# A layer in front of a scan: one affine operation a block into an image in DRAM, and the convolution's row windows loaded from that image

## The chip, the cores and the metric

The kernel runs on one core of a Trainium2 chip. The metric is the device time of one execution in microseconds (us). The core has a matrix engine (PE, whose weight loads are shown apart as PEld), a vector engine (DVE), a scalar engine (ACT), a general engine (POOL), and a queue engine (SP), which here issues nearly all DMA transfers. Each engine works through its own list of instructions in order; between engines, semaphores hold an instruction back until what it needs is there. All data is 32-bit floating point.

## The reference

The input is four images of 128 channels by 128 x 128 pixels. Four layers follow, each `x = x + layer(groupnorm(x))`:

- layer 0, a deformable 3x3 convolution (offsets and a mask from a small convolution, bilinear samples gathered from the image, then a projection);
- layer 1, a dilated 5x7 convolution to 16 channels and two 1x1 convolutions;
- layer 2, described below;
- layer 3, a 3x3 convolution less a term of differences of the channel sum.

Layer 2 is the one that matters here:

```python
x = cf_layernorm(x, pre_w, pre_b)          # over the channels of a pixel
x1, x2 = jnp.split(x, 2, axis=1)           # two halves of 64 channels
x1 = dwconv(x1, dw_w)                      # 3x3, one filter a channel
x2 = ss2d(x2.transpose(0, 2, 3, 1), ...)   # in_proj, 3x3 dwconv, silu, a selective scan
                                           # in four directions, a norm, a gate, out_proj
y = jnp.stack([x1, x2], axis=2).reshape(Bb, 2 * C, a, b)
return cf_layernorm(y, post_w, post_b)
```

The selective scan walks over all 16384 pixels of an image in four orders (by rows, by columns, and both backwards), with 16 states for each of 128 channels. That recurrence is the largest piece of work of the whole program.

## The kernel before

An image is held in DRAM between the layers as 128 channels (partitions) by 16384 pixels. Work goes by blocks of `R = 4` rows, `N = 512` pixels; an image has `NBLK = 32` blocks.

**The scan and what runs beside it.** `scan` is the main loop: for every image, direction and block 16 steps, each one `tensor_tensor_scan` on DVE (L1092) over 128 partitions by 512 pixels, 8192 in all. A step needs a decay `pa`, which ACT computes with one `Exp` from `delta` (`decay`, L979) into one of two or three buffers, and its input `h`, which DVE (three times a block, L949) or POOL (once a block) makes from `du`. POOL multiplies the result with `cb` (`outputs`, L1016), and PE sums it. The tiles `delta`, `du`, `bb` and `cb` are loaded by SP once a block (L929, L936, L955, L961), spread over partitions, from small images in DRAM that the same loop has stored shortly before (`prepare`: `stepsd`, `bcd`).

All other layers of the images run beside that scan. They are Python generators: `weave` takes a list of groups of steps, each with a lag in blocks, and gives one round per block, with a `yield` after every group; the scan pulls so many groups after each of its own steps that both end together. For layer 2's first part this is about two groups a scan step, and a round has 27 groups. This fixes the order of the instructions on each engine when the program is built, and `keep_order` at the end holds it. `store` does not issue a DMA at once: it puts it on a list, and `tick`, called once after every scan step, counts its delay down and issues it on SP; `flush` issues all that wait. Any two DMAs of SP leave in program order, and one that must wait holds those behind it.

**Layer 2's first part, `layer2_pre`**, makes what the scan needs. Per block, with its lag in rounds in brackets:

- `fetch` (0) loads the block `xr`, `centre` (2) subtracts the channel mean with a matmul, `square` (2) copies the result `d` and its square out on ACT, `spread_variance` (3) averages the square over channels with a matmul, `invert` (3) makes the inverse root with `Ln` and `Exp` on ACT, `scale` (3) multiplies `d` by it on POOL (L713).
- `affine(-1)`, `affine(0)`, `affine(1)` (4; L737) apply the norm's weight and bias on ACT and put the result into the convolution's windows. A block has two windows of `R + 2` rows, `a` for the channels of the scan and `b` for the others; each holds its 64 channels twice, in the upper and the lower 64 partitions, one copy being a row further down, so that one matmul over 128 partitions does two rows of filter taps at once. `affine(0)` writes the block's own four rows, `affine(-1)` and `affine(1)` write its first and last row into the windows of the blocks before and after it. Each writes 64 partitions into `a` and 64 into `b`, so an inner block costs six operations on ACT.
- `shift` (5) has SP copy each window's half, `R + 1` rows, into the other half of the partitions, one row further down (L147, `win<-win`).
- `convolve` (6; L762, L765) runs six and three matmuls over the windows, `copy` (6; L774, L778) and `gate` (6; L785) take the results and project the gate `z`, and `finish_strip` (6) applies Silu to two blocks at once, with two loads of ACT's function tables, and stores `u`, `z` and a transposed copy of `u`.

For image 0 the stage starts with nothing beside it, since the scan can't begin before its first blocks are there; for images 1 to 3 it runs beside the scan of the image before.

Of the kernel before, what the change touches and what calls it, by code (L numbers as in the profile page):

```python
# [10 lines left out]
F32 = mybir.dt.float32  # L11
I32 = mybir.dt.int32
U32 = mybir.dt.uint32
AF = mybir.ActivationFunctionType
# [4 lines left out]
P = 128  # L19
H = 128  # L20
W = 128
HW = H * W
R = 4
N = R * W
NBLK = H // R
# [4 lines left out]
HALF = P // 2  # L30
# [17 lines left out]
V_PREW, V_PREB, V_POSTW, V_POSTB, V_CONVB, V_ONW, V_ONB, V_B3 = range(8)  # L48
# [40 lines left out]
MORE = None  # L89


def weave(n, order, ready=lambda t: True):


    total = n + max(step[0] for group in order for step in group if step is not MORE)
    for t in range(total):
        while not ready(t):
            yield None
        left = iter(())
        for k, group in enumerate(order):  # L100
            for step in group:
                if step is MORE:
                    next(left, None)
                elif 0 <= t - step[0] < n:
                    more = step[1](t - step[0])
                    left = left if more is None else more
            yield (t + (k + 1) / len(order)) / total
        for _ in left:
            pass
# [3 lines left out]
def conv_preact_kernel(ctx: ExitStack, tc: tile.TileContext, a: dict, nb: int):  # L113
    nc = tc.nc
# [4 lines left out]
    dram = ctx.enter_context(tc.tile_pool(name="dram", bufs=2, space=DRAM))  # L119
# [3 lines left out]
    def load(pool, src, shape, name, **kw):  # L123
        t = pool.tile(shape, F32, name=name, **kw)
        nc.sync.dma_start(t, src)
        return t

    def bank(which, name):
        return psb.tile([P, N], F32, name=name, tag=f"bank{which}")
# [4 lines left out]
    def store(dst, src, after=3, of=None):  # L134

        waiting.append([after, of, dst, src])

    def stored(of):
        return all(w[1] is not of for w in waiting)
# [9 lines left out]
    def flush():  # L149
        while waiting:  # L150
            nc.sync.dma_start(*waiting.pop(0)[2:])
# [13 lines left out]
    vec = load(const, a["vec"], [P, NVEC], "vec_sb")  # L165

    def col(i):
        return vec[:, i : i + 1]
# [10 lines left out]
    zero = const.tile([P, 2 * P], F32, name="zero")  # L179
# [18 lines left out]
    def slots(n):  # L198
        for _ in range(n):
            yield None  # L200
# [4 lines left out]
    def rows_of(t, y, n):  # L205

        return t[:, y * W : (y + n) * W].rearrange("p (r w) -> p r w", w=W)

    def flat(t):
        return t.rearrange("p r w -> p (r w)")  # L210

    def rsqrt(dst, src, eps):
        nc.scalar.activation(dst, src, AF.Ln, bias=eps)
        nc.scalar.activation(dst, dst, AF.Exp, scale=-0.5)

    def gn_affine(stats, which=0):

        both = bank(which, "pmv")
        mv = small.tile([P, 2], F32, name="mv")
        nc.vector.bn_aggr(mv, stats)  # L220
        yield from slots(2)
        pm = both[:, 0:1]
        nc.tensor.matmul(pm, gmat, mv[:, 0:1], start=True, stop=True)
        yield None
        d = small.tile([P, 1], F32, name="gnd")
        nc.vector.tensor_sub(d, mv[:, 0:1], pm)
        e = small.tile([P, 1], F32, name="gne")
        nc.vector.scalar_tensor_tensor(e, d, d, mv[:, 1:2], ALU.mult, ALU.add)
        yield from slots(2)
        pv = both[:, 1:2]  # L230
        nc.tensor.matmul(pv, gmat, e, start=True, stop=True)
        yield None
        sc = small.tile([P, 1], F32, name="gnscale")
        rsqrt(sc, pv, gn_eps)
        yield None
        sh = small.tile([P, 1], F32, name="gnshift")
        nc.vector.scalar_tensor_tensor(sh, pm, -1.0, sc, ALU.mult, ALU.mult)
        yield None
        return sc, sh
# [4 lines left out]
    def image(name, parts=P):  # L244
        return dram.tile([parts, HW], F32, name=name)
# [404 lines left out]
    def layer2_pre(st):  # L650
        CH = 32
        x2d, stats = st["x2"], st["stats2"]
        zd, yd = image("zd"), image("yd")
        urow, ucol = image("urow"), image("ucol")
        st["z"], st["y1"], st["u"], st["out"] = zd, yd, (urow, ucol), 0
        low = slice(0, HALF)
        with ExitStack() as s:
            wp = s.enter_context(tc.tile_pool(name="l2w", bufs=1))
            pp = s.enter_context(tc.tile_pool(name="l2p", bufs=2))
            inx = load(wp, a["inx"], [P, P], "inx_sb")  # L660
            inz = load(wp, a["inz"], [P, P], "inz_sb")
# [9 lines left out]
            for t in range(6):  # L671
# [2 lines left out]
                nc.vector.tensor_scalar_mul(diag[:, t % 3, half], eye2, dww[:, t : t + 1])  # L674
                yield None
            nc.sync.dma_start(yd[HALF:P, (H - 1) * W :], zero[HALF:P, 0:W])
            sc, sh = yield from gn_affine(stats)

            cms = wp.tile([P, P], F32, name="cms")
# [8 lines left out]
            got = {}  # L688
# [23 lines left out]
                d = got["d", i]  # L712
                nc.gpsimd.tensor_mul(d, d, got.pop(("s", i)))  # L713

            def window(i):

                if ("w", i) not in got:
                    got["w", i] = a, b = [
                        pp.tile([P, R + 2, W], F32, name=f"win{h}", bufs=4) for h in range(2)
                    ]  # L720
                    for edge, row in ((0, 0), (NBLK - 1, R + 1)):
                        if i == edge:
                            nc.gpsimd.memset(a[HALF:P, row, :], 0.0)
                            nc.gpsimd.memset(b[low, row, :], 0.0)
                return got["w", i]

            def affine(to_block):

                to = {0: slice(1, R + 1), -1: slice(R + 1, R + 2), 1: slice(0, 1)}[to_block]
                of = {0: slice(0, R), -1: slice(0, 1), 1: slice(R - 1, R)}[to_block]  # L730

                def one(i):
                    d = got["d", i].rearrange("p (r w) -> p r w", w=W)
                    if not 0 <= i + to_block < NBLK:
                        return
                    for t, part in zip(window(i + to_block), (slice(HALF, P), low)):
                        nc.scalar.activation(  # L737
                            t[part, to, :], d[part, of, :], AF.Identity,
                            bias=vec[part, V_PREB : V_PREB + 1], scale=vec[part, V_PREW : V_PREW + 1],
                        )  # L740

                return one

            def shift(i):
                a, b = got["w", i]
                store(a[low, 1 : R + 2, :], a[HALF:P, 0 : R + 1, :], 2, a)
                store(b[HALF:P, 1 : R + 2, :], b[low, 0 : R + 1, :], 2, b)

            def convolve(i):
                a, b = got["w", i]  # L750
                if not (stored(a) and stored(b)):
                    flush()
                got["u", i] = px = bank(0, "px")
                got["y", i] = py = bank(1, "py")
                px3 = px.rearrange("p (r w) -> p r w", w=W)
                py3 = py.rearrange("p (r w) -> p r w", w=W)
                use = [(1, 0, 0), (0, 0, -1), (2, 0, 1), (4, 1, 0), (3, 1, -1), (5, 1, 1)]
                for n, (t, ty, tx) in enumerate(use):
                    first, final = n == 0, n == len(use) - 1
                    co, cf = span(tx, W)  # L760
                    rf = slice(1 + ty, 1 + ty + R)
                    nc.tensor.matmul(px3[:, :, co], convw[:, t, :], a[:, rf, cf], start=first, stop=final)  # L762
                    yield
                    if ty == 0:
                        nc.tensor.matmul(py3[:, :, co], diag[:, t, :], b[:, rf, cf], start=first, stop=n == 2)  # L765
                        yield
# [15 lines left out]

            def gate(i):
                got["z", i] = pz = bank(2, "pz")
                nc.tensor.matmul(pz, inz, flat(got.pop(("w", i))[0][:, 1 : R + 1, :]), start=True, stop=True)  # L785

            def finish_strip(i):
                j, q = divmod(i, BPB)
# [23 lines left out]
                if (y0 + SB) % CH == 0:  # L812
                    c0 = y0 + SB - CH
                    for q in range(4):
# [3 lines left out]
                            got["c"][:, part, :], 3 + 3 * q,  # L818
                        )

            order = [[(6, convolve), (0, fetch), (2, centre)], [MORE], [MORE], [MORE], [(2, square)],
                     [MORE], [MORE], [(3, spread_variance)], [MORE], [MORE], [(3, invert)], [MORE],
                     [MORE], [(4, affine(-1))], [MORE], [(4, affine(0)), MORE], [(3, scale)], [(5, shift)],
                     [(4, affine(1)), MORE], [(6, copy)], [(6, gate)], [], [(6, finish_strip), MORE], [MORE], [MORE], [MORE], [MORE]]
            yield from weave(NBLK, order)
            flush()
        st["out"] = NBLK + 1
# [575 lines left out]
    def head(b):  # L1403
        st = sts[b]
        table = [(loads(None, layer0_table(st), True), 12)] if b < 2 else []
        return table + [(loads("POOL", layer0(st)), 28), (loads("PE", layer1(st), True), 14),
                (loads("PE", layer2_pre(st), True), 36)]
# [119 lines left out]
```

## Time and profile before

| | |
|---|---|
| three runs, us | 20952.19, 20988.35, 20998.19 (median 20988.35) |
| the profiled execution, us | 20974.44 |
| its span, us | 20972.7 |
| busy: PE, DVE, ACT, POOL, us | 15902.0, 16829.4, 13520.5, 15936.7 |
| moved by DMA, MB (mean GB/s) | 4641.36 (221) |
| first and last `win` operation on ACT | 2171.7 and 16960.6 us |
| `win` operations on ACT | 752, 450.6 us busy |
| `win<-win` copies issued by SP | 256, of 160 KB |

The profile is one execution. The span is the time between its first and last instruction; the profiled execution's own time is 1.7 us longer. Instructions are grouped by line of the code, engine, operation and the tiles they write and read (`out<-in`); behind the bar of a group stand its busy time in us and the mean duration of one in ns, then how long its engine was idle just before such an instruction, and what ended that idle time. In tables of waits the three numbers are the total in us, how many waits, and the longest. `SPq` is SP issuing or waiting to issue a DMA.

### The profile page before, as it was taken

The numbers are of one execution on the slowest core, as the hardware profiler recorded it, in microseconds if no ns is written. First come the engines' busy times: TensorE is split into PE (matmuls) and PEld (weight loads), VectorE is DVE, ScalarE is ACT, GpSimd is POOL, SyncE is SP. The second block draws the span as 40 slices with busy tenths as digits, with TensorE's granted clock in tenths as the row PEclk, the third lists the DMA queues.
The fourth block names the chain that finished last, engine by engine and source line by source line (L and its number), as shares of the span: only waits on it lengthen the run. The fifth ranks groups of instructions, "written<-read, shape, count | busy, mean of one in ns | idle before, by whom it ended". The sixth has DMA issues, their size and how long they took to land.

```text
span 20972.7 us, 208394 instructions
## 1 busy us (share of the span) xinstructions
PE 15902.0 (76%) x58778; PEld 6783.4 (32%) x58778; DVE 16829.4 (80%) x14665; ACT 13520.5 (64%) x26854; POOL 15936.7 (76%) x9469
## 2 busy tenths in 40 slices
PE   4667776777878888777788887877777877677778
PEld 2444222444322223344432222344432222222223
DVE  1222588888998899878799889978889898999993
ACT  3444676677667776666667776666666867655563
POOL 3664577666788888767778888867768889999994
PEclk7888888888989899889898998989988988888899
DMA  7666568777766787777776696777776677555673
GB/s 233 192 193 191 163 201 285 241 258 253 245 195 205 218 236 252 241 250 253 247 237 201 201 253 223 260 237 248 256 233 213 208 209 219 186 184 192 198 219 123
DMA packets 2869279, 4641.36 MB, mean 221 GB/s; under 512 B 1088976, under 2 KB 1361944, under 8 KB 2791200
## 3 DMA queue, kind: packets, MB, share of 16 engines
q1 hardware_dynamic: 2499488, 3419.78, 51.4%
q0 software_dynamic: 368640, 1208.25, 18.7%
q8 instruction: 475, 7.78, 0.2%
q14 instruction: 676, 5.54, 0.1%
HBM read 3682.39 MB, written 874.52 MB: 217 GB/s over the span
## 4 chain that ended last, share of the span: by engine, by line
DVE 35%; PE 21%; ACT 13%; issue 12%; DMA 8%; another core or an unknown queue 5%; POOL 4%; SPq 2%; DVEq 0%; ACTq 0%; POOLq 0%
DVE h L1092 20%; DVE h L949 11%; PE pst L484 5%; PE psum L914 4%; ACT pa L979 4%; ACT g L460 3%; DMA du<-stepsd 3%; PE acc L504 2%; DVE g L473 2%; DMA delta<-stepsd 2%; PE dub L942 1%; PE p L1322 1%; PE yacc L990 1%; POOL h L1016 1%
## 5 line engine op out<-in xcount | busy, mean ns | idle before, releaser
L1092 DVE TENSOR_TENSOR_SCAN h<-pa,carry,h 128x512 f32<-128x512 f32 x8192 | 10017.2, 1267 | 936.8 <-ACT pa L979 704.5
L979 ACT ACTIVATE pa<-delta,neg_a 128x512 f32<-128x512 f32 x8192 | 5532.3, 686 | 4282.6 <-DVE h L1092 3380.0
L1016 POOL TENSOR_TENSOR h<-h,cb 128x2048 f32<-128x2048 f32 x1692 | 7669.8, 4533 | 136.3 <-POOL carry L1010 0.2
L447 POOL DMA_INDIRECT g<-table,idx x4608 | 4811.2, 1044 | 2460.0 <-issue 1525.9
L949 DVE TENSOR_TENSOR h<-du,dub 128x2048 f32<-128x2048 f32 x1625 | 3685.7, 2268 | 924.3 <-PE dub L942 294.7
L484 PE MATMUL pst<-ident,g 128*128 128x128 f32 x18432 | 2685.4, 302 | 1390.1 <-ACT smp L496 623.0
L942 PE MATMUL dub<-u,xb_sb 128*128 128x512 f32 x3250 | 2057.5, 719 | 1789.3 <-DVE h L949 1490.7
L484 PEld LDWEIGHTS pst<-ident,g 128*128 128x128 f32 x18432 | 2369.5, 157 | 2377.0 <-issue 1140.6
L460 ACT ACTIVATE g<-g,wt 128x128 f32<-128x128 f32 x9216 | 2897.4, 392 | 53.7 <-DMA g<-table,idx 51.2
L990 PE MATMUL yacc<-h,gather_sb 128*32 128x512 f32 x16384 | 2363.5, 646 | 88.2 <-POOL h L1016 58.2
L949 POOL TENSOR_TENSOR h<-du,bb 128x2048 f32<-128x2048 f32 x423 | 1928.1, 4558 | 17.9 <-DMA du<-stepsd 16.8
L496 ACT COPY smp<-pst 128x512 f32<-128x512 f32 x1152 | 664.6, 577 | 1731.4 <-remote 1209.5
L473 DVE TENSOR_TENSOR g<-g,wl 128x512 f32<-128x512 f32 x2304 | 1483.5, 670 | 189.0 <-issue 98.7
L921 POOL TENSOR_TENSOR steps<-steps,u 128x512 f32<-128x512 f32 x512 | 652.6, 1275 | 1194.6 <-ACT steps L918 1176.3
L942 PEld LDWEIGHTS dub<-u,xb_sb 128*128 128x128 f32 x3250 | 599.5, 211 | 2956.4 <-DVE h L949 2151.8
L504 PE MATMUL acc<-smp,w_sb 128*128 128x512 f32 x2304 | 1343.7, 666 | 235.6 <-issue 105.7
L1322 PE MATMUL p<-xn,w_l_sb 128*128 128x508 f32 (+2 forms) x2304 | 1146.3, 619 | 1.8 <-ACT xn L1301 1.8
L990 PEld LDWEIGHTS yacc<-h,gather_sb 128*32 128x32 f32 x16384 | 340.2, 111 | 1848.0 <-issue 1325.4
L914 PE MATMUL psum<-e,ident 128*128 128x512 f32 x1024 | 617.7, 688 | 409.9 <-ACT bc L908 354.5
L914 PE MATMUL psum<-one_e,less 128*128 128x512 f32 x1024 | 653.5, 725 | 359.6 <-ACT one_e L910 358.1
L511 DVE TENSOR_TENSOR x<-acc,xres 128x512 f32<-128x512 f32 x128 | 87.4, 683 | 976.9 <-remote 350.2
L1016 DVE TENSOR_TENSOR h<-h,cb 128x2048 f32<-128x2048 f32 x356 | 817.1, 2295 | 12.2
(171 smaller groups left out, 17648.1 us busy)
## 6 DMA issues: line engine op xcount, KB each, us to landing
cb<-bcd SPq DMA_DIRECT2D x512, 1024.0 KB
delta<-stepsd SPq DMA_DIRECT2D x2048, 256.0 KB
du<-stepsd SPq DMA_DIRECT2D x2048, 256.0 KB
stepsd<-steps SPq DMA_DIRECT2D x512, 512.0 KB
table<-gt SPq DMA_DIRECT2D x512, 256.0 KB
bb<-bcd SPq DMA_DIRECT2D x512, 256.0 KB
g<-table,idx POOLq DMA_INDIRECT x4608
u<-urow SPq DMA_DIRECT2D x256, 256.0 KB
```

The lines of the kernel that those rows point to most:

```text
L447: nc.gpsimd.indirect_dma_start(out=g[:, r].rearrange("p q c -> p (q c)"), out_offset=None, in_=table, in_offset=bass.IndirectOffsetOnAxis( ...
L460: nc.scalar.activation(g[:, r, c, :], g[:, r, c, :], AF.Copy, scale=wv[:, 2 * h + r, q, k, c : c + 1])
L473: nc.vector.tensor_mul(g, g, wl.unsqueeze(3).to_broadcast([P, 2, 2, P]))
L484: nc.tensor.matmul(pst[:, r * P : (r + 1) * P], g[:, r % 2, q, :], ident, start=q == 0, stop=q == 3, is_transpose=True,)
L504: nc.tensor.matmul(got["a", i], w0[:, k, :], got.pop(("c", n)), start=k == 0, stop=k == KK - 1)
L914: nc.tensor.matmul(pd, sign, t, start=n == 0, stop=n == 3)
L942: nc.tensor.matmul(p, xb[:, seq[t][1], j, :], c["u"], start=True, stop=True)
L949: engine.tensor_mul(h, c["du"], b.unsqueeze(1).to_broadcast([P, NG, N]))
L979: nc.scalar.activation(pa, blocks[t]["d", g], AF.Exp, scale=neg_a[:, k, at : at + 1])
L990: nc.tensor.matmul(c["y"][g * Q : (g + 1) * Q, :], gather, c["h", j][:, g, :], start=j == 0, stop=last and not second,)
L1016: engine.tensor_mul(h, h, c["cb"][:, j, :].unsqueeze(1).to_broadcast([P, NG, N]))
L1092: nc.vector.tensor_tensor_scan(o, f, o, carry[:, n : n + 1], ALU.mult, ALU.add)
```

## The change

The three affine steps, the windows they write into and the shift copies are replaced. `affine` (now one step, lag 4) applies weight and bias to the whole block on all 128 partitions, in place, with one ACT operation, and stores the block into `nd`, an image in DRAM with a row of zeros above and one below. `windows` (lag 5) loads both windows of a block from `nd`, in two halves each: the rows themselves into one half of the partitions and the rows from one further up into the other. A window has `R + 1` rows instead of `R + 2` and three buffers instead of four, and `convolve` and `gate` index it from 0 instead of 1. The zero rows come from two small DMAs an image, instead of memsets on POOL. `affine` stands in the third group of the round; its first piece stood in the 14th before. `windows` stands in the 12th; `shift` stood in the 18th.

```diff
+        nd = dram.tile([P, (H + 2) * W], F32, name="nd")
...
+            for y in (0, H + 1):
+                nc.sync.dma_start(nd[:, y * W : (y + 1) * W], zero[:, 0:W])
...
-            def window(i):
...
-                        pp.tile([P, R + 2, W], F32, name=f"win{h}", bufs=4) for h in range(2)
...
-                            nc.gpsimd.memset(a[HALF:P, row, :], 0.0)
-                            nc.gpsimd.memset(b[low, row, :], 0.0)
...
-            def affine(to_block):
-
-                to = {0: slice(1, R + 1), -1: slice(R + 1, R + 2), 1: slice(0, 1)}[to_block]
-                of = {0: slice(0, R), -1: slice(0, 1), 1: slice(R - 1, R)}[to_block]
...
-                    for t, part in zip(window(i + to_block), (slice(HALF, P), low)):
-                        nc.scalar.activation(
-                            t[part, to, :], d[part, of, :], AF.Identity,
...
-            def shift(i):
-                a, b = got["w", i]
-                store(a[low, 1 : R + 2, :], a[HALF:P, 0 : R + 1, :], 2, a)
-                store(b[HALF:P, 1 : R + 2, :], b[low, 0 : R + 1, :], 2, b)
+            def affine(i):
+                d = got.pop(("d", i))
+                nc.scalar.activation(d, d, AF.Identity, bias=col(V_PREB), scale=col(V_PREW))
+                store(nd[:, (i * R + 1) * W : ((i + 1) * R + 1) * W], d, 1, nd)
+
+            def windows(i):
+                if not stored(nd):
+                    flush()
+                got["w", i] = a, b = [pp.tile([P, R + 1, W], F32, name=f"win{h}", bufs=3) for h in range(2)]
+                for t, of, own in ((a, slice(HALF, P), slice(HALF, P)), (b, low, low)):
+                    other = low if t is a else slice(HALF, P)
+                    nc.sync.dma_start(t[own], rows_of(nd[of], i * R + 1, R + 1))
+                    nc.sync.dma_start(t[other], rows_of(nd[of], i * R, R + 1))
...
             def convolve(i):
                 a, b = got["w", i]
-                if not (stored(a) and stored(b)):
-                    flush()
...
-                    rf = slice(1 + ty, 1 + ty + R)
+                    rf = slice(ty, ty + R)
...
-                nc.tensor.matmul(pz, inz, flat(got.pop(("w", i))[0][:, 1 : R + 1, :]), start=True, stop=True)
+                nc.tensor.matmul(pz, inz, flat(got.pop(("w", i))[0][:, 0:R, :]), start=True, stop=True)
...
-            order = [[(6, convolve), (0, fetch), (2, centre)], [MORE], [MORE], [MORE], [(2, square)],
-                     [MORE], [MORE], [(3, spread_variance)], [MORE], [MORE], [(3, invert)], [MORE],
-                     [MORE], [(4, affine(-1))], [MORE], [(4, affine(0)), MORE], [(3, scale)], [(5, shift)],
-                     [(4, affine(1)), MORE], [(6, copy)], [(6, gate)], [], [(6, finish_strip), MORE], [MORE], [MORE], [MORE], [MORE]]
+            order = [[(6, convolve), (0, fetch), (2, centre)], [MORE], [(4, affine), MORE], [MORE], [(2, square)],
+                     [MORE], [MORE], [(3, spread_variance)], [MORE], [MORE], [(3, invert)], [MORE, (5, windows)],
+                     [MORE], [], [MORE], [MORE], [(3, scale)], [],
+                     [MORE], [(6, copy)], [(6, gate)], [], [(6, finish_strip), MORE], [MORE], [MORE], [MORE], [MORE]]
```

More of the change, by code (lines that the diff above doesn't have):

```diff
@@ L713, in scale @@
                 nc.gpsimd.tensor_mul(d, d, got.pop(("s", i)))
-            def window(i):
-                if ("w", i) not in got:
-                    got["w", i] = a, b = [
-                        pp.tile([P, R + 2, W], F32, name=f"win{h}", bufs=4) for h in range(2)
-                    ]
-                    for edge, row in ((0, 0), (NBLK - 1, R + 1)):
-                        if i == edge:
-                            nc.gpsimd.memset(a[HALF:P, row, :], 0.0)
-                            nc.gpsimd.memset(b[low, row, :], 0.0)
-                return got["w", i]
@@ L727, in affine @@
-            def affine(to_block):
-                to = {0: slice(1, R + 1), -1: slice(R + 1, R + 2), 1: slice(0, 1)}[to_block]
-                of = {0: slice(0, R), -1: slice(0, 1), 1: slice(R - 1, R)}[to_block]
[L732 to L735, printed above, removed]
-                    for t, part in zip(window(i + to_block), (slice(HALF, P), low)):
-                        nc.scalar.activation(
-                            t[part, to, :], d[part, of, :], AF.Identity,
-                            bias=vec[part, V_PREB : V_PREB + 1], scale=vec[part, V_PREW : V_PREW + 1],
-                        )
-                return one
```

## The prediction

> **What bounds the kernel now.** I read the page's busy times first, then a table of the stretches in which the changed lines run, then, in one of them, who ended the idle time of the engine that carries the scan, and what fills the engine it waits for. The changed stage runs four times, once an image: at about 2150 to 3010 us (the first 165 us of it with no scan beside it) and at 6050, 11040 and 15980 us for about 1050 us each, beside the scan of the image before.
>
> ```profile
> span 20972.7 us, 208394 instructions
> PE 15902.0 (76%) x58778; PEld 6783.4 (32%) x58778; DVE 16829.4 (80%) x14665; ACT 13520.5 (64%) x26854; POOL 15936.7 (76%) x9469
> ...
> core 0: us, PE busy (x) PEld busy (x) DVE busy (x) ACT busy (x) POOL busy (x), PEclk, DMA share, GB/s
> 2150.00:3010.00 860.00, 684.40 (x1848) 245.97 (x1848) 589.69 (x435) 643.00 (x1025) 567.85 (x251) 0.89 0.58 177
> 6050.00:7100.00 1050.00, 841.69 (x2462) 284.67 (x2462) 948.80 (x678) 801.39 (x1284) 895.12 (x383) 0.90 0.64 200
> 11040.00:12100.00 1060.00, 860.33 (x2499) 291.99 (x2500) 939.02 (x676) 818.34 (x1307) 896.29 (x383) 0.90 0.65 203
> 15980.00:17020.00 1040.00, 854.70 (x2493) 289.89 (x2491) 923.62 (x669) 809.68 (x1297) 880.30 (x380) 0.91 0.65 203
> ```
>
> In these stretches DVE is busy 89 to 90% of the time: the scan on DVE is the spine, and only its 101 to 121 us of idle time a stretch can be won. Who ends it, in the second stretch:
>
> ```profile
> DVE h L1092 <- ACT pa L979: 77.3, 84, 3.3
> DVE cols L811 <- ACT u L799: 6.7, 8, 1.1
> DVE h L949 <- PE dub L942: 4.2, 7, 1.4
> ...
> L979 ACT ACTIVATE pa<-delta,neg_a 128x512 f32<-128x512 f32 x558 | 374.0, 685 | 199.6 <-DVE h L1092 179.9 <-DMA delta<-stepsd 18.2 <-DMA xr<-x2d 0.5
> L737 ACT ACTIVATE win<-d,vec_sb 64x128 f32<-64x128 f32 x124 | 60.8, 490 | 2.4
> L737 ACT ACTIVATE win<-d,vec_sb 64x512 f32<-64x512 f32 x63 | 51.1, 811 | 1.2
> ```
>
> Three quarters of the idle time is a scan step waiting for its decay `pa` from ACT; the other stretches say 81.6, 84.4 and 83.4 us, 326.7 us in all. ACT itself has time (it waits 179.9 us for the scan to free a buffer). It is late when other work lies in front of a decay, as here, where two pairs of window operations do:
>
> ```profile
> 6313.40 0.99 ACT L737 ACTIVATE win<-d,vec_sb 64x128 f32<-64x128 f32 x2
> ...
> 6314.30 0.67 ACT L979 ACTIVATE pa<-delta,neg_a 128x512 f32<-128x512 f32 x1
> ...
> 6315.00 1.28 DVE L1092 TENSOR_TENSOR_SCAN h<-pa,carry,h 128x512 f32<-128x512 f32 x1 [0.56 <-ACT pa L979]
> ```
>
> **The change, part by part.** Times are against the profiled execution, 20974.4 us (span 20972.7 us), 14 us under the median of the three runs (20988.4). A measurement can tell about 0.2%, 42 us, from no change.
>
> The affine operations. All 752 window operations go: 256 at 811 ns and 496 at 490 ns, 450.6 us of ACT. In come 128 on 128x512 with bias and scale columns; the row of that very form (`colour`, L1198) has 805 ns, so 103 us. Per full stretch 111.9 us become about 25. To price it on the path I went back from each wait of a scan step for `pa`, along ACT's unbroken work, over three decays: window operations stand in that work for 34.0, 22.9, 27.6 and 27.6 us of waiting, 112 us. The new operation returns 25/112 of it, which leaves 87 us. Lower end 0: ACT's freed time may just lengthen its 179.9 us of waiting. Upper end: the chain of waits in the four stretches gives `ACT win L737` 6.7, 4.3, 4.7 and 5.0%, 205 us, less the same share 160. I take 87, since each piece of it is a wait seen to end there.
>
> The shift copies. Two 160 KB copies inside SBUF a block go, each issued late: the convolution's matmuls wait for them 36.9 us in total (21.5, 1.5, 7.7, 6.2), and the matmuls of the scan queue behind them on PE. The window loads are issued half a round earlier. Laying the changed order of SP over this trace, with 5 us from issue to landing (the copies' own median by their semaphores is 4.7 to 5.0), all land 2.8 us or more ahead of the convolution, most 10. Ends 0 and 37; I take 15, as PE is not the spine.
>
> The rounds with no scan beside them. There a round of the pipeline (13 us) is closed by ACT: six window operations (3.67 us), then `u`, `yt`, `z`, while PE idles 2.39 us until `z`. Without them `z` follows `pz`, some 1.7 us earlier; the new operation lies in the 1.22 us that ACT waits for `pd`, and only in rounds with Silu does it cost its 0.8. Ten rounds by 1.3 are 13 us. Ends 0 and 17.
>
> What moves. The affine operation is now 11 groups earlier in its round, nearer to POOL's `scale` (L713), which it needs. Counting decays up to its new place in ACT's order, POOL was done 4 to 24 us before ACT got there in every block beside the scan, so this wait costs nothing; if that cover went, every decay behind it on ACT would wait too. The edge memsets (16 by 0.2 us) go unpriced, off the path. The order of everything else on PE, DVE, POOL and SP is the same instruction for instruction.
>
> SP's queue. A block issues one store and four loads in place of two copies: 392 more issues with the two edge stores an image, of 0.5 to 0.6 us. The first load waits until the store has landed, and all that is behind it on SP waits too. The row for a store to DRAM that is read back at once:
>
> ```profile
> SPq L955 <- POOL carry L1010: 179.2, 29, 9.8
> SPq L936 <- DVE h L949: 142.6, 31, 8.3
> SPq L929 <- DMA stepsd<-steps: 73.6, 23, 5.4
> ```
>
> The third line is that row, 3.2 us a wait and 5.4 at most. The first two say why it is mostly hidden: SP stands waiting for POOL and DVE with `bb` and `du` anyway. By the changed order laid over the trace, the loads wait 1.5 us on the mean, and the next old transfer goes out 0.4 us late on the mean, 49 us over 120 blocks. Ends 0 and 49; I take 10, as only 9 of 139 `delta` loads in the stretch were felt by ACT.
>
> [...]
>
> Bytes. 576 KB more a block of 30 us, 19 GB/s on 200, the DMA share from 0.64 to about 0.70. Other stretches of this trace run at 0.75 and more, so there is room, but transfers land later: ACT's waits for `delta` are 33.0, 18.2, 15.8 and 14.4 us, 29 in number. With 0.4 us on each, 12 us. Ends 0 and, if these waits doubled, 81.
>
> Sum: -87 - 15 - 13 + 10 + 12 = -93, so 20881 us. All the good ends together give -214 (20760), all the bad ones +130 (21104).
>
> **The rivals.** First, the chain is right and not the direct waits: an operation less on ACT shortens what later waits inherit (POOL's wait for ACT `steps`, 97.5 us in the second stretch, too). That is the good end, 20760. For it speaks that ACT and DVE hand on to each other at every step; against it, that a wait saved is often given back at the next hand-over.
>
> Second, the change does little: a scan waits for ACT's other bursts as well (Silu with its two table loads, 4.7 us in a row; the step-size operations), and the one removed only uncovers the next. Then just the rounds without a scan and the costs are left, -13 + 10 + 12: 20983.
>
> Third, slower: `delta` loads stuck behind the window loads. In 65 of 120 blocks the next transfer on SP is a `delta` load, and the last two of a block are needed a few scan steps after their issue. A stop is 3.2 us plus three more issues, 5.0 us; were all 65 felt, 325 us. The gain of 115 us is gone when a third of them are. With half felt: 20974 - 115 + 12 + 163 = 21034. Against it stand the waits of SP for POOL and DVE.
>
> Fourth, the four half loads take turns. Issued 0.6 us apart, the two half copies of now land within 5 us each, side by side. If four went one after the other (4 by 4.7 us), 60 of 119 blocks would miss their convolution, by 152 us in total: 21033 if PE hands on all of it. This is what the Trainium skill (DMA: Bandwidth & Descriptors, "Rules for kernel authors") says of two transfers to disjoint partition halves, that they serialize and one of 128 partitions is better; the copies in the trace do not show it at this size.
>
> **How the numbers follow.** Forecast 0.50 (its own range 20800 to 20940), the larger gain 0.14, no change 0.20, late `delta` loads 0.11, halves in turn 0.05. Faster by over 0.2% (below 20946) are the first two, 0.64; within it the third, 0.20; slower the last two, 0.16. The range runs from 20740, just past the good end, to 21020, which leaves out the full forms of the two slow cases.
>
> **What would show it.** ACT's `win` groups are replaced by one of 128 operations near 805 ns; ACT is busy about 85 us less in each later stretch; scan steps wait some 55 to 65 us for `pa` in place of 77 to 84; the convolution's wait for `win` is near zero; the stretches are 20 to 30 us shorter. SP shows waits of window loads for the `nd` store of some 50 us a stretch. I am wrong if ACT's waits for `delta`, or DVE's for `du`, grow by more than 30 us a stretch, if ACT waits for POOL `d` ahead of the affine operation, or if the scan's waits for `pa` stay where they were although ACT is less busy.

## The result, and the profile after

Five runs of the changed kernel took 20850.08 to 20898.84 us, median 20873.01; five of the kernel before on the same chip 20952.19 to 20998.19 us, median 20981.72. The ratio is 0.9945 with a 95% interval of 0.9934 to 0.9956: 109 us less. The profiled execution took 20873.0 us. The busy times of its page, in the order of those shown of before:

```profile
span 20871.2 us, 208527 instructions
PE 15906.6 (76%) x58778; PEld 6786.0 (33%) x58778; DVE 16828.5 (81%) x14665; ACT 13184.7 (63%) x26230; POOL 15930.9 (76%) x9453
```

DVE, POOL and PE are busy as long as they were, within 6 us; ACT has 335.8 us and 624 operations less. The saving lies in the four stretches in which the stage runs. The table of stretches, cut at the same scan steps in both kernels (columns as in the table before: length, then busy time of PE, PEld, DVE, ACT and POOL, the granted clock, the DMA share, GB/s):

```profile
2154.00:2965.90 811.90, 669.00 (x1843) 238.94 (x1843) 583.74 (x424) 560.44 (x869) 568.53 (x247) 0.91 0.68 211
5997.30:7024.20 1026.90, 838.06 (x2457) 279.84 (x2459) 940.85 (x678) 718.18 (x1126) 895.18 (x379) 0.91 0.71 222
10968.20:12005.30 1037.10, 849.75 (x2499) 288.81 (x2498) 943.41 (x676) 734.39 (x1149) 893.20 (x379) 0.92 0.72 225
15892.40:16916.70 1024.30, 842.02 (x2493) 285.45 (x2491) 927.87 (x669) 727.53 (x1142) 879.60 (x376) 0.92 0.72 225
```

The same scan steps took 856.6, 1049.8, 1058.6 and 1040.7 us before, so the stretches are 44.7, 22.9, 21.5 and 16.4 us shorter, 105.5 in all; the three parts between them moved by -7.5, +2.7 and +7.3 us, which shows how far a part can move that was not changed. DVE's work in the four is the same, 3399 us before and 3396 after; what went is its idle time. PE is busy 40 us less in them, with the same matmuls, and the granted clock there is 0.91 to 0.92 where it was 0.89 to 0.91. Who ended DVE's idle time, in the second stretch (total us, times, longest):

```profile
DVE h L1073 <- ACT pa L960: 56.0, 58, 3.1
DVE h L930 <- DMA du<-stepsd: 7.1, 2, 4.6
...
DVE h L930 <- PE dub L923: 3.0, 4, 1.2
```

The scan's waits for the decay fell from 77.3 to 56.0 us there, and a wait for the `du` load, which was not in the list before, has come in. Over all four stretches, before and after, in us:

| who waits for what | before | after |
|---|---|---|
| DVE, scan step for ACT `pa` | 326.7 | 215.6 |
| DVE, `h` for PE `dub` | 30.7 | 18.8 |
| DVE, `cols` for ACT `u` | 163.2 | 153.0 |
| DVE, `h` for the `du` load | 34.8 | 69.9 |
| ACT, `pa` for the `delta` load | 81.4 | 206.5 |
| PE, convolution for `win` | 36.9 | 4.6 |

The four lines of DVE give 111 + 12 + 10 - 35, 98 of the 105.5 us. The fifth is the largest change and hardly shows in the time: ACT still waits for the scan to free a buffer far longer than for `delta`, here in the second stretch:

```profile
ACT pa L960 <- DVE h L1073: 214.9, 169, 5.2
ACT pa L960 <- DMA delta<-stepsd: 49.6, 21, 10.9
```

The one operation a block that came in, in the groups of ACT by line and shape (count, then busy us and mean ns, then idle time before it and what ended it):

```profile
L720 ACT ACTIVATE d<-d,vec_sb 128x512 f32<-128x512 f32 x128 | 102.7, 803 | 4.2 <-POOL d L716 4.2
```

And the queue's own waits on SP in the second stretch. The first line is a wait that the prediction does not have: SP stands at the store to `nd` (L147) until ACT has made `d`. The second is the wait of a `delta` load for the store of `stepsd` to land, 73.6 us before. The last is the wait of the first window load for the store to `nd` to land, which the prediction does have:

```profile
SPq L147 <- ACT d L720: 62.7, 23, 7.8
...
SPq L910 <- DMA stepsd<-steps: 35.5, 18, 4.7
...
SPq L729 <- DMA nd<-d: 12.9, 6, 4.1
```

### The profile page after: what moved, and what is told of

The parts are those of the page before. It is cut to its first block, busy times and chain, and to the rows that moved or that the text cites. A ratio compares the mean times of both kernels' runs of the same rounds, so it can differ in the third digit from the quotient of the medians.

```text
span 20871.2 us, 208527 instructions
## 1 busy us (share of the span) xinstructions
PE 15906.6 (76%) x58778; PEld 6786.0 (33%) x58778; DVE 16828.5 (81%) x14665; ACT 13184.7 (63%) x26230; POOL 15930.9 (76%) x9453
## 4 chain that ended last, share of the span: by engine, by line
DVE 35%; PE 21%; issue 11%; ACT 11%; DMA 9%; another core or an unknown queue 5%; POOL 3%; SPq 3%; DVEq 0%; POOLq 0%; ACTq 0%
DVE h L1073 20%; DVE h L930 11%; PE pst L484 5%; PE psum L895 4%; DMA du<-stepsd 3%; ACT pa L960 3%; ACT g L460 3%; PE acc L504 2%; DVE g L473 2%; PE dub L923 2%; DMA delta<-stepsd 2%; PE yacc L971 2%; PE p L1303 1%; DMA g<-table,idx 1%
```

## The experiments

Twelve runs in three groups, each group on one chip with its own runs of the kernel before. The chips differ (the kernel before took 20207.15, 20214.72 and 20902.18 us on them), so each saving is the median against that of the kernel before beside it; where two kernels of one group are compared with each other, it is said. "Four stretches" is the sum of a wait over the four, as in the table above. The profiles of groups 1 and 2 are read against those of group 2's own two: there the kernel before has 323, 38 and 32 us of DVE's waits for `pa`, `dub` and `du`, and the changed kernel 217, 18 and 71.

| kernel | ratio, 95% interval | median, us | saved, us |
|---|---|---|---|
| group 1: ACT's load put back | 0.9980 [0.9971, 0.9989] | 20168.56 | 39 |
| before, without the halo rows | 0.9948 [0.9934, 0.9961] | 20107.69 | 99 |
| store later | 0.9936 [0.9923, 0.9950] | 20077.03 | 130 |
| twice the loads | 0.9980 [0.9970, 0.9990] | 20169.35 | 38 |
| group 2: the kernel before again | 1.0000 [0.9990, 1.0010] | 20212.62 | 2 |
| the changed kernel again | 0.9935 [0.9922, 0.9949] | 20091.79 | 123 |
| by way of SBUF | 0.9944 [0.9930, 0.9957] | 20101.92 | 113 |
| before, window work earlier | 0.9982 [0.9973, 0.9991] | 20175.37 | 39 |
| group 3: the changed kernel, third time | 0.9944 [0.9931, 0.9958] | 20783.19 | 119 |
| store later, again | 0.9939 [0.9925, 0.9952] | 20763.29 | 139 |
| store a little later | 0.9935 [0.9922, 0.9949] | 20757.13 | 145 |
| four more loads, of one row | 0.9970 [0.9958, 0.9981] | 20834.93 | 67 |

### The kernels themselves, again

No edit: the kernel before as a twin for itself, and the changed kernel beside the others.

> The kernel before once more, for a profile on the same chip as the experiments beside it. Every theory expects a ratio of 1.000 within 0.002 and, by stretch of scan steps, what the first profile showed, shifted where the chip's clock or transfers differ.

> The changed kernel once more, on the same chip as the experiments beside it. A ratio of 0.9945 within 0.0015 is expected by every theory; the loads-twice run at 0.998 then prices the extra loads at 0.35%, some 70 us, and ACT's load put back at the same.

> The changed kernel again, beside the two versions with a later store, so that they are compared on one chip and against the same runs of the kernel before. A ratio of 0.9935 to 0.9945 by every theory.

The saving is 123 and 119 us on the two chips. The twin of before differs from it by 2 us, and the intervals reach 18 to 29 us to either side, so a difference of 40 us from the kernel before is told, and one of 10 to 20 between two kernels is not. The changed kernel of group 2, second stretch, who ended DVE's idle time:

```profile
DVE h L1073 <- ACT pa L960: 55.4, 56, 3.2
DVE h L930 <- DMA du<-stepsd: 8.7, 3, 5.7
...
DVE h L930 <- PE dub L923: 2.6, 4, 1.2
```

### ACT's load put back into the changed kernel

```diff
+            def again(rows, n, inside=lambda i: True):   
+                        nc.scalar.activation(idle[1][part, rows, :], idle[0][part, rows, :], AF.Identity, ...)
-                     [MORE], [], [MORE], [MORE], [(3, scale)], [],
-                     [MORE], [(6, copy)], ...
+                     [MORE], [(4, again(one_row, 2, ...))], [MORE], [(4, again(all_rows, 1)), MORE], [(3, scale)], [],
+                     [(4, again(one_row, 2, ...)), MORE], [(6, copy)], ...
```

Five operations a block, of the shapes that were taken away and in their old places; with the one at L720 ACT has as many operations as before (26854, 13605.4 us busy against 13606.4). Transfers are those of the changed kernel.

> The changed kernel with ACT's old load put back: at the three old places in the round ACT runs dummy affine operations of the old shapes on scratch tiles (two rows of 64x128, one 64x512, two of 64x128), so that with the new operation a block costs ACT about 3.6 us as before. The output does not change; the DRAM image and the window loads stay. Theory A (the gain is ACT's freed time in front of the decays): the scan's waits for pa go back to about 80 us in each later stretch, and the time to that of before plus what the transfers cost, 20975 to 21010 us. Rival B (the gain is that the windows arrive early and PE no longer waits for the shift copies): the time stays at 20870 to 20890 us.

It saves 39 us where the changed kernel of group 2 saves 123 (the kernel before is within 0.04% of the same time on these two chips): some 84 us of the change are ACT's load, with intervals of 18 us on the one and 27 us on the other. DVE's waits for `pa` are 304 us over the four stretches, of 323 before and 217 after. Second stretch, DVE:

```profile
DVE h L1088 <- ACT pa L975: 67.2, 84, 3.0
DVE cols L807 <- ACT u L795: 6.7, 8, 1.1
DVE h L945 <- DMA du<-stepsd: 5.5, 2, 3.2
DVE h L945 <- PE dub L938: 4.3, 6, 1.5
```

But 39 us remain with all of ACT's work back, so there is a second cause in the rest of the change: the transfers, and the earlier place of the window work.

### The kernel before without its halo rows

```diff
+            kept = [[wp.tile([P, R + 2, W], F32, name=f"win{h}k{n}") for h in range(2)] for n in range(4)]
-                     [MORE], [(4, affine(-1))], [MORE], [(4, affine(0)), MORE], [(3, scale)], [(5, shift)],
-                     [(4, affine(1)), MORE], [(6, copy)], ...
+                     [MORE], [], [MORE], [(4, affine(0)), MORE], [(3, scale)], [(5, shift)],
+                     [MORE], [(6, copy)], ...
```

The four one-row operations a block are left out (the convolution sees zeros there); the copies inside SBUF and their place are those of before.

> The kernel before with the four small window operations a block left out (its halo rows stay zero in four fixed pairs of windows, so the convolution misses the rows of the neighbour blocks), transfers as before. ACT loses 1.96 us a block where the change takes 2.78 us. Theory A: 70% of the change's 111 us fewer waits for pa, 78 us, and some 8 us in the rounds without a scan: about 20895 us, and more than the change gives per us of ACT, as no transfer is added. Rival B: 20960 to 21000 us, since the shift copies and PE's waits for them stay.

It saves 99 us with 221.6 us less of ACT, and DVE's waits for `pa` fall from 323 to 251 us over the four stretches. DVE in the second stretch:

```profile
DVE h L1090 <- ACT pa L977: 63.9, 65, 3.1
...
DVE h L947 <- PE dub L940: 4.1, 6, 1.4
```

The wait for `dub` stays (43 us over the four stretches, 38 before), and no wait for `du` comes in (35, 32 before). So less work on ACT shortens one wait, and nothing of the transfers is needed for it. The saving is 20 us more than was expected; the waits for `pa` and `cols` (163 to 152 us) account for 83 of the 99 us, and the rest was not traced.

### The kernel before with its window work earlier

```diff
-            order = [[...], [MORE], [MORE], [MORE], [(2, square)],
-                     [MORE], [MORE], [(3, spread_variance)], [MORE], [MORE], ...
-                     [MORE], [(4, affine(-1))], [MORE], [(4, affine(0)), MORE], [(3, scale)], [(5, shift)],
-                     [(4, affine(1)), MORE], ...
+            order = [[...], [MORE], [(4, affine(-1)), MORE], [MORE], [(4, affine(0)), (2, square)],
+                     [MORE], [MORE], [(4, affine(1)), (3, spread_variance)], [MORE], [(5, shift), MORE], ...
+                     [MORE], [], [MORE], [MORE], [(3, scale)], [],
+                     [MORE], ...
```

Same operations, same copies; only their groups in the round change, to about where the changed kernel has its own.

> The kernel before with the same six window operations and two shift copies a block, all issued some 9 to 11 groups earlier in the round (3rd, 5th and 8th group, the copies in the 10th): ACT's load and the transfers are those of before, and only the windows arrive earlier. Theory B (part of the gain is PE no longer waiting for late windows): PE's waits for win vanish and the time falls by about 40 us, what the run with ACT's load put back kept, 0.998. Theory A alone: within 10 us of before, 0.9995 to 1.0005.

It saves 39 us. DVE in the second stretch of the kernel before in this group, and then of this kernel:

```profile
DVE h L1092 <- ACT pa L979: 75.1, 83, 3.3
...
DVE h L949 <- PE dub L942: 4.6, 6, 1.6
```

```profile
DVE h L1092 <- ACT pa L979: 82.8, 76, 2.7
...
DVE h L949 <- PE dub L942: 0.2, 1, 0.2
```

Over the four stretches the waits for `dub` go from 37.7 to 9.8 us and PE's wait for `win` from 30 to 1, while those for `pa` stay in sum (320): over the three later stretches they are 49 us shorter at the thirteenth step of a block, where the window operations stood, and 50 us longer at the other steps. So a second cause is the place in the round, which this run moves for ACT's operations and the copies at once.

It is tempting to join the two: the convolution that waits for late windows would hold the scan's matmuls behind it on PE. The trace doesn't bear that out. Of the 31 waits for `dub` in this group's kernel before, only 3, with 7.0 of the 37.7 us, come at the end of a run of matmuls that began with a wait for `win`; in the first profile of before it is 2 of 28, with 2.3 of 30.7 us. Most (21, with 23.1 us) end a run that began with the step-size matmuls `psum`, released by ACT's `one_e`. The longest of those in the last stretch, and the same scan step in this kernel, on PE (start, length, group) and for DVE:

```profile
15930.29 2.08 PE L914 MATMUL psum<-one_e,less 128*128 128x512 f32 x2 [2.84 <-ACT one_e L910]
...
15943.75 1.02 PE L942 MATMUL dub<-u,xb_sb 128*128 128x512 f32 x2
...
15944.81 2.29 DVE L949 TENSOR_TENSOR h<-du,dub 128x2048 f32<-128x2048 f32 x1 [2.34 <-PE dub L942]
```

```profile
15893.79 1.12 PE L914 MATMUL psum<-one_e,less 128*128 128x512 f32 x2 [2.64 <-ACT one_e L910]
...
15904.50 1.02 PE L942 MATMUL dub<-u,xb_sb 128*128 128x512 f32 x2
```

The order on PE is the same in both, but the first matmuls of the run take about twice as long in the kernel before, and `dub` starts 13.5 us after the start of the run in place of 10.7. Of the some 1010 `psum` matmuls in the four stretches, 217 take over 1.0 us in the kernel before, 117 in this one and 136 in the changed kernel; the others mostly take 0.59. So slower matmuls on PE are a rival to late windows for the second cause. Why fewer of them are slow when the window work stands earlier, no run here shows.

### By way of SBUF in place of DRAM

```diff
-                nc.scalar.activation(d, d, AF.Identity, bias=col(V_PREB), scale=col(V_PREW))
-                store(nd[:, (i * R + 1) * W : ((i + 1) * R + 1) * W], d, 1, nd)
+                        nc.scalar.activation(ring(i + to_block)[:, to, :], d[:, of, :], AF.Identity, ...)
...
-                    nc.sync.dma_start(t[own], rows_of(nd[of], i * R + 1, R + 1))
-                    nc.sync.dma_start(t[other], rows_of(nd[of], i * R, R + 1))
+                    store(t[of], o[of, 1 : R + 2, :], 1, t)
+                    store(t[other], o[of, 0 : R + 1, :], 1, t)
```

The affine result goes into a ring of tiles in SBUF, with two more ACT operations a block for its first and last row (128 partitions, 485 ns), and four copies inside SBUF make the windows. There is no store to DRAM and no wait for one to land.

> The round trip through DRAM taken out: the affine operation writes all 128 partitions into a ring tile of R+2 rows in SBUF (one 128x512 and two 128x128 operations a block, 1.8 us of ACT where the change has 0.8 and before had 3.6), and four copies inside SBUF fill the windows at the same place in the round. No store, no wait for its landing, 640 KB a block where the change moves 896 and before 320. Theory A alone: 64% of the freed ACT time, so 64% of the change's fewer waits for pa, and a gain of 70 us, 0.9965. Theory S or T on top (stop at the store, bytes): DVE's waits for du and ACT's for delta fall to near those of before, and the gain is 90 us or more, 0.9955 or below.

It saves 113 us, 10 less than the changed kernel beside it, with 94 us more of ACT (13366.9 against 13272.5); the intervals overlap. Its waits are 237 us for `pa` and 50 for `du`, against 217 and 71. So the way through DRAM is no visible loss against this one; that its longer waits for `du` cost about what its shorter `pa` waits bring would account for it.

### The store issued later

```diff
-                store(nd[:, (i * R + 1) * W : ((i + 1) * R + 1) * W], d, 1, nd)
+                store(nd[:, (i * R + 1) * W : ((i + 1) * R + 1) * W], d, 4, nd)
-                     ..., [(3, invert)], [MORE, (5, windows)],
-                     [MORE], [], [MORE], [MORE], [(3, scale)], [],
+                     ..., [(3, invert)], [MORE],
+                     [MORE], [], [MORE], [MORE], [(3, scale)], [(5, windows)],
```

The store goes out four scan steps after the affine operation in place of one, when ACT has made `d`, and the window loads later to suit. In the version "a little later" it is three steps, and the loads sit in the fifteenth group.

> The changed kernel with the store of the nd image issued four scan steps after the affine operation instead of one, and the window loads six groups later (18th group of the round). It tells apart two causes for the later delta and du transfers. Theory S (SP stands at the nd store until ACT has done the affine operation, and holds delta and du back): SP's wait for ACT d falls from 283 us to under 100, ACT's wait for delta in the four stretches from 206 to under 130, DVE's for du from 70 to about 45, and the time to about 20845 us. Theory T (the added bytes slow all transfers): nothing of this moves, 20865 to 20880 us. If the later loads come too late, PE waits for win again, and it is 20890 us or more.

> The version with the store four scan steps after the affine operation and the window loads in the 18th group, again. By its profile the four stretches are 27 us shorter than the changed kernel's on the same chip: 0.13% under the changed kernel beside it. If that was one execution's scatter, the two are equal within 0.05%.

> As before it, but with the store three scan steps after the affine operation and the loads in the 15th group, so that PE's 21 us of waiting for late windows (13 of them in the first stretch) should go while SP still does not stand at the store. Theory S: as fast as the version with four steps or up to 10 us faster; if SP stands at the store again for over 100 us, between that one and the changed kernel.

The wait that was not foreseen goes. SP in the second stretch of the changed kernel of group 2 and of the store four steps later:

```profile
SPq L147 <- ACT d L720: 64.2, 24, 7.8
```

```profile
SPq L147 <- ACT d L720: 13.1, 7, 4.5
```

Over the four stretches it is 292 us in the changed kernel, 45 with four steps and 84 with three. The time hardly follows: against the changed kernel beside them in group 3 the two save 20 and 26 us, and in group 1 the saving is 7 more than that of the changed kernel in group 2. All three go the same way, but it is 0.03 to 0.13%, and the intervals overlap with the changed kernel's. ACT's waits for `delta` fall to 160 us and DVE's for `du` to 51, where under 130 and about 45 were expected. So some 200 us and more of standing on SP are worth, by the medians, at most some 26 us: SP stands a little later at the `bb` or `du` load instead (its wait for POOL `carry` in the second stretch is 148.4 us in place of 127.2). All its waits of the four stretches together are 2053 us in group 2's changed kernel and 2018 with four steps, 2041 and 2018 in group 3. With three steps the kernel is the fastest of those run, by a margin that these runs can't settle.

### More loads on SP

```diff
+                for h, part in enumerate((low, slice(HALF, P), low, slice(HALF, P))):
+                    if h % 2 == 0:
+                        c = pp.tile([P, R + 1, W], F32, name=f"spare{h}", bufs=1)
+                    nc.sync.dma_start(c[part], rows_of(x2d[part], min(i * R, H - R - 1), R + 1))
```

Behind the four window loads four more of the same shape, 160 KB each, into tiles that nobody reads. The other version loads one row by each, 32 KB (`c[part, 0:1]`): as many issues, a fifth of the bytes.

> The changed kernel with four more loads of 160 KB a block from x2d into spare tiles that nobody reads, right behind the window loads: 640 KB and four issues more a block, more than the change itself added in bytes (576 KB). Theory T (bytes and issues cost): DVE's waits for du grow by another 35 us or more over the four stretches, and the time is 20905 to 20940 us. Theory S (the cost is SP's stop at the store): 20873 to 20890 us.

> The changed kernel with four more loads a block as in the loads-twice run, but of one row each: 32 KB instead of 160, the same number of issues on SP. It tells apart why the loads-twice run lost 78 us against the changed kernel: if it was the bytes, this one loses about a fifth, 15 us (0.9943 where the changed kernel has 0.9935); if it was the issues and SP's waits for a free slot of its eight, it loses most of it, 50 us or more.

The large ones leave a saving of 38 us out of 123, the small ones 67 out of 119: 85 and 52 us lost for 512 loads. Second stretch, DVE and then ACT, of the changed kernel of group 3 and then of the kernel with four small loads:

```profile
DVE h L930 <- DMA du<-stepsd: 7.3, 2, 5.8
...
ACT pa L960 <- DMA delta<-stepsd: 51.0, 19, 11.6
```

```profile
DVE h L934 <- DMA du<-stepsd: 17.8, 5, 7.4
...
ACT pa L964 <- DMA delta<-stepsd: 85.4, 31, 13.6
```

Over the four stretches ACT's waits for `delta` are 322 us with the large and 318 with the small loads, 186 and 206 without; DVE's for `du` 102 and 108, without 71 and 65 (both of these profiled executions lie 20 to 27 us above their medians). In both versions the last two `delta` loads of a block leave SP 5.1 and 4.3 us ahead of the first scan step of that block (from the ends of their issues to the start of that step, a mean over the three later stretches); in the changed kernel it is 6.1 and 5.1, before it 7.2 and 6.1. A fifth of the bytes does the same to the order and to these waits, so the larger part of the price is that SP issues one by one, some 0.6 us each; SP's waits for transfers to land grow only from 323 to 351 us with the small ones. What the bytes add is between nothing and 33 us: the two versions ran on different chips, and this is not settled.

## Why the prediction was right

The forecast was 20881 us against a profiled 20974.4, a gain of 93; the profiled execution of after took 20873, a gain of 101. By the medians it is 109. The chain of reasons held in its main term. The size of the second term and the price of the transfers stay open, so that the sum came out within some 16 us is in part luck.

**The affine operations, -87.** Right, though no closer than the intervals allow. Putting them back costs 84 us, and the scan's waits for `pa` fall by 111 us in the traces of the prediction's own chip and by 106 in group 2's. The marker was 55 to 65 us a later stretch; 56.0, 55.2 and 53.4 came. The row for 128 partitions was right too (805 ns from `colour`, 803 measured), and ACT is busy 83 us less a later stretch where 85 were named. The halo rows alone, 243 us or 70% of the 348 us that ACT was to lose, give 72 of the 106 us of `pa` waits, 68%: a share by busy time held. The reading that DVE is busy 89 to 90% holds for the three later stretches; in the first it is 69% (590 of 860 us), and that one gave most, 44.7 us.

**The shift copies, -15.** Open. The wait of 36.9 us for `win` is PE's, and "as PE is not the spine" is borne out as far as it goes: only 2.3 us of DVE's waits for `dub` begin with it. But the place of the window work in the round, ACT's operations and the copies together, is worth 39 us by itself (18 to 55 by its interval), and DVE's waits for `dub` fall by 28 us with it; in the changed kernel they fall by 12 us in the first traces and by 20 in group 2's. The prediction showed the line of `dub` (4.2 us in the second stretch, of 30.7 in the four) and gave it no term. What shortens it is not known; the trace points to PE's slow `psum` matmuls rather than to late windows.

**The rounds with no scan, -13.** From the start of the stage to the first scan step it took 159.1 us before and 149.0 after, -10.

**SP's queue and bytes, +22.** The mechanism was right, and the size not fully told. DVE's waits for `du` rise by 35 to 39 us and ACT's for `delta` by 125 (from 81.4 to 206.5; by 116 in group 2). Of the second, little reaches the scan, since ACT has 190 to 215 us of waiting for DVE in each later stretch. What the transfers cost in time was not run by itself. The 52 us for 512 small loads would put the 392 issues that the change adds at 40 us (an estimate by the count, 392/512 of 52). With ACT's load put back the kernel saves 39 us, no less than the one that only moves the window work, which would put the price near 0; but in the traces of the three later stretches the first has 19 us of waits for `du` and is 6 us shorter than before, the second has 3 and is 24 us shorter. 22 lies between 0 and 40, and that is not settled.

**The waits of SP that were named.** The loads were to wait some 50 us a stretch for `nd` to land; it is 9 to 13 in the later ones (33.7 in the first). In its place SP stands 283 us over the four stretches at the store, because `store` lets one scan step pass and ACT reaches the operation later. The prediction counted the store as an issue and not as a wait for ACT: this was overlooked, though the same kind of line, the queue's `bb` load waiting for POOL, was shown. It cost little, as the later store shows. From the start of its issue to its landing the store takes 3.2 us on the median of all 128 (3.8 in the second stretch), worked out from its semaphore, and SP waits for it 35 times. The Trainium skill (DMA: Bandwidth & Descriptors, "Anatomy of one DMA") has a fit for a DMA that the general engine issues, 2.0 us plus its bytes over 436 GB/s, by which 256 KB take an estimated 2.6 us; this store is issued by SP, which the fit does not cover.

**The markers for being wrong.** One of them came about: ACT's waits for `delta` grew by 31, 40 and 40 us in the later stretches, over the 30 named, and the forecast held all the same. It was badly set: an engine with 190 us of slack can take on 30 us of waiting and pass none of it on. POOL's `d` ahead of the affine operation cost 4.2 us in all, so that cover held. The last stretch is 16.4 us shorter, where 20 to 30 were forecast.

**The rivals.** That the change does little is ruled out by the two runs that take and give work of ACT, -99 and +84. That the saving runs on through the chain (20760) did not come: the gain is what the direct waits say, and a part was given back at the `du` loads, as it was said against it. `delta` loads behind the window loads are real, as ACT's waits and the shrunken lead show, but the rival asked that half of 65 stops be felt by the scan; what DVE felt was 35 us of `du`. The halves in turn are not seen: PE waits 4.6 us for `win` in the whole execution, where four transfers one after the other were to give 152. The Trainium skill (DMA: Bandwidth & Descriptors, "Rules for kernel authors") advises one transfer of 128 partitions in place of two to disjoint halves, since those serialize; no run here loads a window in one transfer. What the runs do show is that each transfer costs its issue on SP: 52 us for 512, where the bytes of the larger ones add between nothing and 33 us.

## What to carry to other kernels

Price an operation on a side engine by the waits of the spine in whose unbroken run of work it stands; that gave 87 where 84 was measured, while its busy time alone (336 us less) says nothing. When an engine off the spine waits, look at what of the spine's own work is queued behind it there, and follow each wait of the spine back to where the run of work before it began: the totals of `dub` and `win` fell together here, and hardly any `dub` wait began with a wait for `win`. And count a queue's price in issues that have to leave in order, and ask of each store whether its data is ready when the queue gets to it.

## What the runs showed that was not expected

- SP's standing at the store is 283 to 292 us over the four stretches, and with 200 to 247 of it gone the kernel gains 7 to 26 us: a queue that stands in one place would else mostly have stood at the next, and all its waits together fall by 9 to 36 us.
- Four loads of 32 KB a block cost 52 us and four of 160 KB 85, and both push the last two `delta` loads of a block 1.0 and 0.8 us nearer to their use.
- The way through DRAM and the way inside SBUF differ by 10 us, though the first has a store to land before four loads may go.
- The step-size matmuls on PE run slow (over 1.0 us where most take 0.59) 217 times in the four stretches of the kernel before and 117 times with the window work earlier, though their order is the same.
